# Layer 1's feed-forward network of a two-layer decoder, put into one written order

## The chip, the core and the metric

The kernel runs on one core of a Trainium2 chip. Such a core has engines that work side by side, each through a queue of its own, in order: TensorE (PE in the profile; PEld is its weight load), VectorE (DVE), ScalarE (ACT), GpSimd (POOL), and SyncE (SP), which issues the DMA transfers. They wait for one another through semaphores. Data lie in SBUF (128 partitions); matmul results go to PSUM, which DVE and ACT read and POOL does not touch in this kernel.

The metric is the device time of one execution in microseconds (us), lower is better. Before the change it is 2464.19 us, the median of three runs (2464.09 to 2467.39).

## What is computed

A decoder of two layers on x of shape (2, 1024, 256): six sublayers, each followed by a residual addition and a layernorm without weights. The change concerns the last sublayer, a SwiGLU network of width 704 with fake-quantised activations and weights:

```python
def _act_fake_quant(x, clip_factor):
    scale = sigmoid(clip_factor) * max(abs(x)) / 127.0      # one scale for the whole tensor
    return clip(round(x / scale), -128.0, 127.0) * scale
...
xq = _act_fake_quant(x, clip_x[0])
gate = einsum('bsh,ih->bsi', xq, _weight_fake_quant(w_gate))
up = einsum('bsh,ih->bsi', xq, _weight_fake_quant(w_up))
h = _act_fake_quant(silu(gate) * up, clip_down[0])
return einsum('bsi,hi->bsh', h, _weight_fake_quant(w_down))
...
x = _layernorm(x + _L1_ffn_ref(x, ...))
```

Two maxima over whole tensors cut this into stages: nothing of the network can start before the largest |x| is known, and no part of h can be quantised before the largest |h| is.

## The kernel before

The 2048 tokens are four groups of 512 (`NG = 4`, `GT = 512`); a group lies as four tiles of 128 tokens by 256. The quantised weights were made ready much earlier (`wgu`, `wdT`, with integers in bf16), and the scales are multiplied in afterwards.

**The end of the cross-attention** (`l1_xattn`). Token tiles n = 0 to 15 go through a pipeline of steps: softmax, turning, mixing with the values, turning back, output projection. `output` (L1625 on) adds the residual into `res[g]` (L1637) and normalises a group in two parts, three tiles when the third is there and one at the end: bn_stats and aggregate on DVE (L178, L179), variance plus epsilon (L181), a power of -1/2 on POOL (L183), the scaling on DVE (L200), then the part's largest |x| into a column of `xm` (L1644). Only PE's order is written by hand there.

**The maximum of x** (`whole_scale`, L1679 to L1693): a maximum on DVE, a transpose on PE, a second maximum, a broadcast by a matmul, a scalar operation and a reciprocal.

**Gate and up** (L1730 to L1755). `quantised(g)` rounds a group in two halves: ACT multiplies by the reciprocal scale and adds 12582912, which rounds to an integer (L1718), and two DVE operations clip from both sides and give bf16 (`integers`, L1709 and L1710). Eight transposes on PE (L1724) and two copies (`evac`, L70 on DVE and L74 on ACT) give `xqT`. Then six chunks of 128 hidden features (the last has 64): four matmuls of 512 columns into a PSUM tile of two banks (`wide`, two buffers), gate into one bank and up into the other (L1738); silu on ACT with gate's scale (L1743); on DVE the product of up, its scale and the silu into `h` (L1747), and the chunk's largest |h| into a column of `hm` (L1751). `quantised(g + 1)` stands behind chunk 2 in the program. The order of the instructions on every engine is a planner's here, which may pull ready work ahead.

**Quantise and down** (L1756 to L1780). After `whole_scale` for h, each group: per chunk ACT rounds (L1768), DVE clips in two operations (L1709, L1710) into `hq`, PE multiplies four token tiles with 256 columns of `wdT` (L1771), summing over the six chunks into two `wide` tiles, of which half the columns are used. Then DVE multiplies the four sums by `srow` (L1777), POOL adds x (L1779, in the last group DVE), and `layernorm` follows: statistics on DVE, power on POOL, an offset on DVE (L191), four scaled tiles on ACT (L196). `store` (L1784) sends the group's 512 KB to memory from SP's queue.

Of the kernel before, what the change touches and what calls it, by code (L numbers as in the profile page):

```python
# [9 lines left out]
F32 = mybir.dt.float32  # L10
# [8 lines left out]
P = 128  # L19
B, S, D = 2, 1024, 256  # L20
T = B * S
NG = 4
# [11 lines left out]
class Decoder:  # L34
# [1493 lines left out]
    def l1_xattn(self):  # L1528
# [11 lines left out]
        self.xm = self.late.tile([P, 2 * NG], F32, name="xm")  # L1540
        with ExitStack() as s:
# [84 lines left out]
            def output(n):  # L1626
# [11 lines left out]
                if i == 2:  # L1638
                    new[g] = self.xp.tile([P, 4, D], F32, tag="x", name="xg")
                tiles = {2: range(3), 3: range(3, 4)}.get(i)  # L1640
                if tiles:
                    self.normalise(new[g], res[g], tiles)
                    k = 2 * g + i - 2
                    nc.vector.tensor_reduce(  # L1644
                        self.xm[:, k : k + 1], new[g][:, tiles.start : tiles.stop, :], AX.XY, ALU.max,
                        apply_absolute_value=True,
                    )
# [22 lines left out]
    def l1_ffn(self, out):  # L1670
# [4 lines left out]
        with ExitStack() as s:  # L1675
# [36 lines left out]
            def quantised(g):  # L1712

                v = self.rp.tile([P, 4, D], F32, tag="r", name="r")
                xq = two.tile([P, 4, D], BF16, name="xq")
                for k in range(0, 4, 2):
                    i = slice(k, k + 2)
                    nc.scalar.activation(v[:, i, :], self.x[g][:, i, :], AF.Identity, bias=magic, scale=rx)  # L1718
                    integers(xq[:, i, :], v[:, i, :])
                xqT = two.tile([P, 2, GT], BF16, name="xqT")  # L1720
                for c in range(2):
                    ps = self.ps_t.tile([P, 1024], BF16, tag="t", name="bankb")
                    for i in range(4):
                        nc.tensor.transpose(  # L1724
                            ps[:, i * P : (i + 1) * P], xq[:, i, c * P : (c + 1) * P], self.identb
                        )
                    self.evac(xqT[:, c, :], ps[:, 0:GT])
                return xqT

            xqT = quantised(0)  # L1730
            for g in range(NG):
                now = xqT
                for c in range(NI):
                    n = rows(c)
                    ps = self.wide()
                    for k, wT in enumerate((wgT, wuT)):
                        for d in range(2):
                            nc.tensor.matmul(  # L1738
                                ps[0:n, k, :], lhsT=wT[:, d, c * P : c * P + n], rhs=now[:, d, :],
                                start=d == 0, stop=d == 1,  # L1740
                            )
                    sl = two.tile([P, GT], F32, name="sl", bufs=3)
                    nc.scalar.activation(  # L1743
                        sl[0:n, :], ps[0:n, 0, :], AF.Silu, scale=sg[0:n, c : c + 1]
                    )
                    hv = h[0:n, c, g * GT : (g + 1) * GT]
# [3 lines left out]
                    k = c * NG + g  # L1750
                    nc.vector.tensor_reduce(  # L1751
                        hm[0:n, k : k + 1], hv, AX.X, ALU.max, apply_absolute_value=True
                    )
                    if c == 2 and g + 1 < NG:
                        xqT = quantised(g + 1)  # L1755
            sh, rh = whole_scale(hm, 1, "wsh")  # L1756
            nc.vector.tensor_scalar(self.srow, self.srow, sh, None, ALU.mult)

            for g in range(NG):
                hq = self.weight(None, 1, 2048)[:, 0, :].bitcast(BF16)[:, 0 : NI * GT].rearrange(  # L1760
# [80 lines left out]
```

## Time and profile before

| what | time |
|---|---|
| three runs, median (lowest to highest) | 2464.19 us (2464.09 to 2467.39) |
| the profiled execution | 2464.71 us |
| its span, first to last instruction | 2462.9 us |
| mean granted TensorE clock | 0.982 |
| up to the last tile's scaled x, all other sublayers | to 2369.6 us |
| FFN, from the maximum of x to that of h | 2369.6 to 2413.1 us |
| FFN, quantise and down, to the last group's first product with srow | 2413.1 to 2450.6 us |
| last group's layernorm and store | 2450.6 to 2462.9 us |

How to read the lines of the profile: an engine, a line of the program (a helper's line stands for all its callers: L70 and L74 are `evac`, L183 and L200 the layernorm), an operation, the tile written and the tiles read, shapes as partitions x elements with type, a count. In a timeline the first two numbers are the start and the length in us; instructions of one line that follow each other are merged, so that "2.08 ... x4" are four in 2.08 us together, and as they are pipelined each is longer than a fourth of it. In brackets stands how long the engine was idle before, and what it waited for. In a table of stretches each engine has its busy time and its number of instructions, PEclk is the granted share of TensorE's clock, then come the DMA engines' share and rate. A summary of one line of the program gives a count and the shortest, median and longest duration in ns.

Over the whole span PE is busy 2331.8 us (95%), DVE 1677.5 us, ACT 1110.8 us and POOL 911.3 us. In the FFN stages it is otherwise: between 2369.6 and 2413.1 us PE is busy 29.16 us and DVE 38.51 us.

### The profile page before, as it was taken

The numbers are of one execution on the slowest core, as the hardware profiler recorded it, in microseconds if no ns is written. First come the engines' busy times: TensorE is split into PE (matmuls) and PEld (weight loads), VectorE is DVE, ScalarE is ACT, GpSimd is POOL, SyncE is SP. The second block draws the span as 40 slices with busy tenths as digits, with TensorE's granted clock in tenths as the row PEclk, the third lists the DMA queues.
The fourth block names the chain that finished last, engine by engine and source line by source line (L and its number), as shares of the span: only waits on it lengthen the run. The fifth ranks groups of instructions, "written<-read, shape, count | busy, mean of one in ns | idle before, by whom it ended". The sixth has DMA issues, their size and how long they took to land. (4 is left out here: it accounts for less than half of the span.)

```text
span 2462.9 us, 37293 instructions
## 1 busy us (share of the span) xinstructions
PE 2331.8 (95%) x14062; PEld 1580.2 (64%) x14065; DVE 1677.5 (68%) x2916; ACT 1110.8 (45%) x1730; POOL 911.3 (37%) x747
## 2 busy tenths in 40 slices
PE   7999999999998999999999999999989999999974
PEld 3545545444545668899999999999734444444742
DVE  6888887888785334555555555545788687885786
ACT  4665565565563322233333333333156555664344
POOL 4666666566565222342343332332210001002412
PEclk9999999999999999999999999999999999999986
DMA  7888788688787001010010010100212121210001
GB/s 160 174 159 169 148 169 166 131 161 170 151 172 187 1 1 41 1 39 27 13 35 30 18 41 6 48 1 1 49 25 42 28 40 30 47 23 1 1 1 35
DMA packets 275667, 168.78 MB, mean 69 GB/s; under 512 B 47560, under 2 KB 262176, under 8 KB 275488
## 3 DMA queue, kind: packets, MB, share of 16 engines
q1 hardware_dynamic: 239072, 148.05, 28.6%
q10 hardware_dynamic: 36416, 18.36, 3.7%
q8 instruction: 111, 1.82, 0.3%
q14 instruction: 68, 0.56, 0.1%
HBM read 34.21 MB, written 2.10 MB: 15 GB/s over the span
## 5 line engine op out<-in xcount | busy, mean ns | idle before, releaser
L312 DVE TENSOR_REDUCE nm<-wide 128x1 f32<-128x1024 f32 x256 | 300.7, 1214 | 63.2 <-PE wide L297 62.3
L1186 DVE TENSOR_REDUCE most<-bank 128x1 f32<-128x512 f32 x476 | 300.4, 684 | 25.3 <-PE bank L1176 17.3
L1229 ACT ACTIVATE w<-wide 128x1024 f32<-128x1024 f32 x256 | 248.3, 1022 | 147.0 <-PE wide L1223 138.8
L297 PE MATMUL wide<-k,q 64*128 64x512 f32 x1024 | 271.5, 627 | 18.8 <-ACT p L317 17.4
L328 POOL TENSOR_SCALAR p<-p,sums 128x1024 f32<-128x1024 f32 x128 | 143.6, 1121 | 269.6 <-DVE sums L325 269.6
L379 PE MATMUL acc<-turned,v 128*64 128x256 f32 x2048 | 235.1, 382 | 2.2 <-ACT aoT L74 1.7
L379 PEld LDWEIGHTS acc<-turned,v 128*64 128x64 f32 x2048 | 142.6, 137 | 113.6 <-issue 30.7
L906 ACT ACTIVATE mhT<-mhT,cols 128x256 f32<-128x256 f32 (+1 forms) x256 | 143.3, 607 | 147.4 <-DVE mhT L934 105.0
L317 ACT ACTIVATE p<-wide,nm 128x1024 f32<-128x1024 f32 x128 | 142.8, 1116 | 144.9 <-DVE nm L312 118.2
L817 POOL TENSOR_TENSOR hs<-hs,mhT 128x1024 f32<-128x1024 f32 x31 | 102.5, 3307 | 241.6 <-DVE hs L815 241.6
L342 DVE STREAM_TRANSPOSE blocks<-p 128x1024 f32<-128x1024 f32 x128 | 158.0, 1234 | 43.0 <-DMA turned<-blocks 13.3
L297 PEld LDWEIGHTS wide<-k,q 64*128 64x128 f32 x1024 | 89.9, 187 | 146.1 <-issue 76.5
L183 POOL TENSOR_TENSOR rstd<-ve,nhalf 128x4 f32<-128x4 f32 (+2 forms) x28 | 26.1, 934 | 424.7 <-DVE ve L181 424.3
L917 PE MATMUL unit<-xT,w 128*128 128x256 f32 x768 | 182.3, 380 | 0.0
L974 DVE SCALAR_TENSOR_TENSOR r<-acc,gates,r 128x128 f32<-128x128 f32 x256 | 77.7, 345 | 140.4 <-PE acc L965 140.4
L342 DVE STREAM_TRANSPOSE blocks<-r 128x1024 f32<-128x1024 f32 x128 | 153.8, 1202 | 0.0
L917 PEld LDWEIGHTS unit<-xT,w 128*128 128x128 f32 x768 | 140.9, 190 | 16.9 <-issue 0.3
L328 POOL TENSOR_SCALAR r<-r,sums 128x1024 f32<-128x1024 f32 x128 | 143.6, 1122 | 0.0
L317 ACT ACTIVATE r<-wide,nm 128x1024 f32<-128x1024 f32 x128 | 142.2, 1111 | 1.1 <-DVE nm L312 0.9
L1243 PE MATMUL acc<-w,v 128*32 128x512 f32 x1024 | 137.2, 608 | 0.0
L1176 PE MATMUL bank<-kst,qst 64*128 64x512 f32 x476 | 125.9, 459 | 11.8 <-DVE most L1186 11.8
L362 POOL COPY turned<-blocks 32x1024 f32<-32x1024 f32 x128 | 132.0, 1031 | 4.0 <-DVE blocks L342 0.3
(333 smaller groups left out, 4479.3 us busy)
## 6 DMA issues: line engine op xcount, KB each, us to landing
turned<-blocks SPq DMA_DIRECT2D x636, 128.0 KB, 2.8
turned<-blocks ACTq DMA_DIRECT2D x132, 128.0 KB, 3.1
w<-in_L_ffn_W SPq DMA_DIRECT2D x16, 1024.0 KB, 5.3
q<-q SPq DMA_DIRECT2D x64, 128.0 KB, 2.3
k<-k SPq DMA_DIRECT2D x32, 128.0 KB, 2.6
qst<-qh SPq DMA_DIRECT2D x48, 64.0 KB, 2.4
qst<-ql SPq DMA_DIRECT2D x48, 64.0 KB, 2.4
kst<-kh SPq DMA_DIRECT2D x48, 64.0 KB
```

The lines of the kernel that those rows point to most:

```text
L297: nc.tensor.matmul(sc[h][:, kb, :], lhsT=q[rows, qi, at : at + P], rhs=k[rows, ki, :], start=True, stop=True,)
L312: nc.vector.tensor_reduce(nm, sc, AX.XY, ALU.max, negate=True)
L317: nc.scalar.activation(p, sc.rearrange("p a c -> p (a c)"), AF.Exp, bias=nm, accum_out=sums[:, 0, h : h + 1],)
L328: nc.gpsimd.tensor_scalar(p, p, sums[:, 1, h : h + 1], 1.0, ALU.mult, ALU.mult)
L342: nc.vector.transpose(blocks[m][:, :, h, qt, :], p.rearrange("p (j q) -> p j q", q=32))
L362: nc.gpsimd.tensor_copy(b, a)
L379: nc.tensor.matmul(av[own[h], 0:256].rearrange("p (t i q) -> p i t q", t=2, i=4), lhsT=vals[u][:, kt, own[h]], rhs=p[:, h], start=kt == 0, ...
L906: nc.scalar.activation(hT[:, f, cols], hT[:, f, cols], AF.Relu, bias=self.cols[:, col : col + 1])
L917: nc.tensor.matmul(v[:, m, :], lhsT=up[e][k][:, f : f + P], rhs=self.halves[g][k], start=k in (1, 2, 5) and m == 0, stop=True, skip_group_ ...
L1186: nc.vector.tensor_reduce(most[n][:, kb, qt, h : h + 1], sc[a], AX.X, ALU.max, negate=True)
L1229: nc.scalar.activation(slot[:, k, :], ps[k].rearrange("p a q -> p (a q)"), AF.Exp, scale=0.25)
L1243: nc.tensor.matmul(mixed[n][o : o + 32, :], lhsT=vals[b][:, kt, 17 * h : 17 * h + 32], rhs=pT[:, a, :], start=kt == 0, stop=kt == 7, tile_ ...
```

## The change

1. **Cross-attention's end.** The last group is normalised in three parts (two tiles, one, one) instead of two; `xm` has a ninth column.
2. **One written order.** All of the FFN's instructions on PE, DVE, ACT and POOL, from the first rounding to the last layernorm, are issued in the program's order.
3. **Rounding x.** `quantised(g)` becomes `rounded` (ACT; in groups 1 to 3 also one clip from both sides on POOL), `clipped` (DVE: in those groups one operation that subtracts 12582912 and gives bf16) and `turned` (transposes, copy of the first half on DVE, of the second on ACT). For group g + 1 the six parts stand behind the six chunks of group g.
4. **Shared products.** In two of six chunks (1 and 4; in the last group 0 and 2) ACT scales up from PSUM into `h` and POOL multiplies by the silu, instead of one DVE product. The chunk's maximum stands two chunks later in all groups (`late`).
5. **Down.** The sums of a group take one `wide` tile. The previous group's `finish` is spread over the six chunks: products and adds (0, 1), statistics (2, 3), scaling and store of two tiles each (4, 5).
6. **Tail.** In the last group POOL adds x to two tiles and DVE to two, the statistics begin with the latter, ACT scales the first half and DVE the second; every group is stored in two DMAs of 256 KB.

```diff
-        self.xm = self.late.tile([P, 2 * NG], F32, name="xm")
+        self.xm = self.late.tile([P, 2 * NG + 1], F32, name="xm")
...
                 nc.vector.tensor_tensor(res[g][:, i, :], ps, self.x[g][:, i, :], ALU.add)
-                if i == 2:
-                    new[g] = self.xp.tile([P, 4, D], F32, tag="x", name="xg")
-                tiles = {2: range(3), 3: range(3, 4)}.get(i)
+                parts = {2: range(3), 3: range(3, 4)}
+                if g == NG - 1:
+                    parts = {1: range(2), 2: range(2, 3), 3: range(3, 4)}
+                tiles = parts.get(i)
                 if tiles:
+                    if tiles.start == 0:
+                        new[g] = self.xp.tile([P, 4, D], F32, tag="x", name="xg")
                     self.normalise(new[g], res[g], tiles)
-                    k = 2 * g + i - 2
+                    k = 2 * NG if i == 1 else 2 * g + i - 2
                     nc.vector.tensor_reduce(
                         self.xm[:, k : k + 1], new[g][:, tiles.start : tiles.stop, :], AX.XY, ALU.max,
                         apply_absolute_value=True,
...
                 nc.vector.tensor_scalar(out, v, MAGIC + QMAX, MAGIC, ALU.min, ALU.subtract)
                 nc.vector.tensor_scalar(out, out, -QMAX - 1.0, None, ALU.max)
...
+            vs, xqs, xqTs = {}, {}, {}
+            def rounded(g, k):
+                if k == 0:
+                    vs[g] = self.rp.tile([P, 4, D], F32, tag="r", name="r")
+                    xqs[g] = two.tile([P, 4, D], BF16, name="xq")
+                i = slice(2 * k, 2 * k + 2)
+                nc.scalar.activation(
+                    vs[g][:, i, :], self.x[g][:, i, :], AF.Identity, bias=magic, scale=rx
+                )
+                if g:
+                    v = vs[g][:, i, :]
+                    nc.gpsimd.tensor_scalar(v, v, MAGIC + QMAX, MAGIC - QMAX - 1.0, ALU.min, ALU.max)
+            def clipped(g, k):
+                i = slice(2 * k, 2 * k + 2)
+                if g:
+                    nc.vector.tensor_scalar(xqs[g][:, i, :], vs[g][:, i, :], MAGIC, None, ALU.subtract)
+                else:
+                    integers(xqs[g][:, i, :], vs[g][:, i, :])
+            def turned(g, c):
+                if c == 0:
+                    xqTs[g] = two.tile([P, 2, GT], BF16, name="xqT")
+                ps = self.ps_t.tile([P, 1024], BF16, tag="t", name="bankb")
+                for i in range(4):
+                    nc.tensor.transpose(
+                        ps[:, i * P : (i + 1) * P], xqs[g][:, i, c * P : (c + 1) * P], self.identb
+                    )
+                self.evac(xqTs[g][:, c, :], ps[:, 0:GT], by=nc.scalar if c else nc.vector)
+            shared = lambda g, c: c in ((0, 2) if g == NG - 1 else (1, 4))
+            late = []
+            def largest(g, c):
+                n, k = rows(c), c * NG + g
+                nc.vector.tensor_reduce(
+                    hm[0:n, k : k + 1], h[0:n, c, g * GT : (g + 1) * GT], AX.X, ALU.max,
+                    apply_absolute_value=True,
+                )
+            def hidden(g, c):
+                n = rows(c)
+                ps = self.wide()
+                for k, wT in enumerate((wgT, wuT)):
+                    for d in range(2):
+                        nc.tensor.matmul(
+                            ps[0:n, k, :], lhsT=wT[:, d, c * P : c * P + n], rhs=xqTs[g][:, d, :],
+                            start=d == 0, stop=d == 1,
                         )
...
+                sl = two.tile([P, GT], F32, name="sl", bufs=3)
+                nc.scalar.activation(sl[0:n, :], ps[0:n, 0, :], AF.Silu, scale=sg[0:n, c : c + 1])
+                hv = h[0:n, c, g * GT : (g + 1) * GT]
+                if shared(g, c):
+                    nc.scalar.activation(hv, ps[0:n, 1, :], AF.Identity, scale=su[0:n, c : c + 1])
+                    nc.gpsimd.tensor_tensor(hv, hv, sl[0:n, :], ALU.mult)
+                else:
                     nc.vector.scalar_tensor_tensor(
                         hv, ps[0:n, 1, :], su[0:n, c : c + 1], sl[0:n, :], ALU.mult, ALU.mult
                     )
...
+            hqs, sums, res, mvs, rstds = {}, {}, {}, {}, {}
+            def quantised(g, c):
+                n = rows(c)
+                hv = h[0:n, c, g * GT : (g + 1) * GT]
+                if c == 0:
+                    hqs[g] = self.weight(None, 1, 2048)[:, 0, :].bitcast(BF16)[:, 0 : NI * GT].rearrange(
+                        "p (c q) -> p c q", c=NI
+                    )
+                nc.scalar.activation(hv, hv, AF.Identity, bias=magic[0:n, :], scale=rh[0:n, :])
+                integers(hqs[g][0:n, c, :], hv)
+            def down(g, c):
+                n = rows(c)
+                if c == 0:
+                    sums[g] = self.wide().rearrange("p a (i d) -> p (a i) d", d=D)
                 for i in range(4):
+                    nc.tensor.matmul(
+                        sums[g][:, i, :], lhsT=hqs[g][0:n, c, i * P : (i + 1) * P],
+                        rhs=self.wdT[0:n, c, :], start=c == 0 and i % 2 == 0, stop=True,
+                        skip_group_check=True,
+                    )
+            def added(g, i, by):
+                if i == 0:
+                    res[g] = self.rp.tile([P, 4, D], F32, tag="r", name="r")
+                r = res[g][:, i, :]
+                nc.vector.tensor_tensor(r, sums[g][:, i, :], self.srow, ALU.mult)
+                by.tensor_tensor(r, r, self.x[g][:, i, :], ALU.add)
+            def weighed(g, i):
+                if g not in mvs:
+                    mvs[g] = self.sm.tile([P, 4, 2], F32, tag="mv", name="mv")
+                st = self.sm.tile([P, 6], F32, tag="st", name="st")
+                nc.vector.bn_stats(st, res[g][:, i, :])
+                nc.vector.bn_aggr(mvs[g][:, i, :], st)
+            def powers(g):
+                ve = self.sm.tile([P, 4], F32, tag="ve", name="ve")
+                nc.vector.tensor_scalar(ve, mvs[g][:, :, 1], EPS, None, ALU.add)
+                rstds[g] = self.sm.tile([P, 4], F32, tag="rstd", name="rstd")
+                nc.gpsimd.tensor_tensor(rstds[g], ve, self.nhalf, ALU.pow)
+            def written(g, half):
+                i = slice(2 * half, 2 * half + 2)
+                if half == 0:
+                    self.x[g] = self.xp.tile([P, 4, D], F32, tag="x", name="xg")
+                by = nc.vector if half and g == NG - 1 else nc.scalar
+                self.scaled(
+                    self.x[g], res[g], range(2 * half, 2 * half + 2), mvs[g][:, i, :],
+                    rstds[g][:, i], by,
+                )
+                b, h = divmod(g, 2)
+                nc.sync.dma_start(
+                    out[b, h * GT : (h + 1) * GT, :].rearrange("(i p) d -> p i d", p=P)[:, i, :],
+                    self.x[g][:, i, :],
+                )
+            def finish(g, c):
+                if c < 2:
+                    for i in range(2 * c, 2 * c + 2):
+                        added(g, i, nc.gpsimd)
+                elif c < 4:
+                    for i in range(2 * c - 4, 2 * c - 2):
+                        weighed(g, i)
+                    if c == 3:
+                        powers(g)
+                else:
+                    written(g, c - 4)
+            engines = {
+                mybir.EngineType.PE, mybir.EngineType.DVE, mybir.EngineType.Activation,
+                mybir.EngineType.Pool,
+            }
+            with self.tc.manual_schedule(engines=engines):
+                for k in range(2):
+                    rounded(0, k)
+                    clipped(0, k)
+                for c in range(2):
+                    turned(0, c)
+                for g in range(NG):
+                    for c in range(NI):
+                        hidden(g, c)
+                        late.append((g, c))
+                        while len(late) > 2:
+                            largest(*late.pop(0))
+                        if g + 1 < NG:
+                            if c < 2:
+                                rounded(g + 1, c)
+                            elif c < 4:
+                                clipped(g + 1, c - 2)
+                            else:
+                                turned(g + 1, c - 4)
+                while late:
+                    largest(*late.pop(0))
+                sh, rh = whole_scale(hm, 1, "wsh")
+                steps = [(g, c) for g in range(NG) for c in range(NI)]
+                for n, (g, c) in enumerate(steps):
+                    quantised(g, c)
+                    if n == 0:
+                        nc.vector.tensor_scalar(self.srow, self.srow, sh, None, ALU.mult)
+                    down(g, c)
+                    if g:
+                        finish(g - 1, c)
+                g = NG - 1
+                for i in range(4):
+                    added(g, i, nc.gpsimd if i < 2 else nc.vector)
+                for i in (2, 3, 0, 1):
+                    weighed(g, i)
+                powers(g)
+                for half in range(2):
+                    written(g, half)
```

Of the lines taken away, those of the FFN are left out here: they are `quantised`, the two loops over groups and `store`, printed above.

More of the change, by code (lines that the diff above doesn't have):

```diff
@@ L1710, in integers @@
                 nc.vector.tensor_scalar(out, out, -QMAX - 1.0, None, ALU.max)
[L1712 to L1725, printed above, removed]
-                        )
-                    self.evac(xqT[:, c, :], ps[:, 0:GT])
-                return xqT
@@ L1730, in l1_ffn @@
[L1730 to L1746, printed above, removed]
+            vs, xqs, xqTs = {}, {}, {}
@@ L1749, in l1_ffn @@
                     )
-                    k = c * NG + g
-                    nc.vector.tensor_reduce(
-                        hm[0:n, k : k + 1], hv, AX.X, ALU.max, apply_absolute_value=True
-                    )
[L1754 to L1760, printed above, removed]
-                    "p (c q) -> p c q", c=NI
-                )
-                ps = [self.wide(), self.wide()]
-                sums = [ps[i // 2][:, i % 2, 0:D] for i in range(4)]
-                for c in range(NI):
-                    n = rows(c)
-                    hv = h[0:n, c, g * GT : (g + 1) * GT]
-                    nc.scalar.activation(hv, hv, AF.Identity, bias=magic[0:n, :], scale=rh[0:n, :])
-                    integers(hq[0:n, c, :], hv)
-                    for i in range(4):
-                        nc.tensor.matmul(
-                            sums[i], lhsT=hq[0:n, c, i * P : (i + 1) * P], rhs=self.wdT[0:n, c, :],
-                            start=c == 0, stop=c == NI - 1,
-                        )
-                r = self.rp.tile([P, 4, D], F32, tag="r", name="r")
-                for i in range(4):
-                    nc.vector.tensor_tensor(r[:, i, :], sums[i], self.srow, ALU.mult)
-                    by = nc.vector if g == NG - 1 else nc.gpsimd
-                    by.tensor_tensor(r[:, i, :], r[:, i, :], self.x[g][:, i, :], ALU.add)
-                self.store(out, g, self.layernorm(r, nc.scalar))
@@ L1782, in store @@
-    def store(self, out, g, x):
-        b, h = divmod(g, 2)
-        self.nc.sync.dma_start(
-            out[b, h * GT : (h + 1) * GT, :].rearrange("(i p) d -> p i d", p=P), x
-        )
+            hqs, sums, res, mvs, rstds = {}, {}, {}, {}, {}
[5 more added lines that the diff above has]
+                        "p (c q) -> p c q", c=NI
+                    )
+                nc.scalar.activation(hv, hv, AF.Identity, bias=magic[0:n, :], scale=rh[0:n, :])
+                integers(hqs[g][0:n, c, :], hv)
```

## The prediction

> **What bounds the kernel now.** The change reaches only the last 97 us of the span, so I read the stage table of those first, then the chain of waits through them, then the timeline row by row. The stages are layer 1's FFN up to the whole-tensor maximum (A: quantise x, gate and up products), from there to the last down product (B), and the tail.
>
> ```profile
> core 0: us, PE busy (x) PEld busy (x) DVE busy (x) ACT busy (x) POOL busy (x), PEclk, DMA share, GB/s
> 2369.60:2413.10 43.50, 29.16 (x128) 12.98 (x131) 38.51 (x74) 25.50 (x37) 0.00 (x0) 0.88 0.00 1
> 2413.10:2450.60 37.50, 21.31 (x98) 12.44 (x99) 25.56 (x96) 23.25 (x36) 11.51 (x15) 0.65 0.10 33
> 2450.60:2462.90 12.30, 0.44 (x3) 0.00 (x0) 4.75 (x18) 2.07 (x4) 1.01 (x1) 0.50 0.22 73
> ```
>
> DVE is busy 89% of A while POOL does nothing: that is what the change works on. But a busy share is not a bound. The timeline of A's last group shows the loop behind it:
>
> ```profile
> 2404.49 0.59 PE L1738 MATMUL wide<-xqT,w_gateT 128*128 128x512 bf16 x2 [0.70 <-DVE h L1747]
> 2405.55 0.69 ACT L1743 ACTIVATE sl<-wide,sc_w_gate 128x512 f32<-128x512 f32 x1 [1.04 <-remote]
> 2406.40 1.49 DVE L1747 SCALAR_TENSOR_TENSOR h<-wide,sc_w_up,sl 128x512 f32<-128x512 f32 x2
> 2407.18 0.59 PE L1738 MATMUL wide<-xqT,w_gateT 128*128 128x512 bf16 x2 [0.81 <-DVE h L1747]
> 2407.80 1.27 DVE L1751 TENSOR_REDUCE hm<-h 128x1 f32<-128x512 f32 x2
> ```
>
> A chunk's silu starts 1.06 after its first matmul, the product 0.85 later, and the matmuls that reuse its PSUM buffer 0.78 after that: 2.69 for a buffer, two buffers, 1.35 a chunk. DVE's own work is about the same (0.66 a product and 0.59 a maximum, spaced as in these rows). So A is bound by latency as much as by DVE, and what counts in a fixed order is who waits behind whom.
>
> In B, ACT and DVE wait on each other around each layernorm:
>
> ```profile
> 2427.28 0.16 DVE L191 SCALAR_TENSOR_TENSOR off<-mv,rstd 128x4 f32<-128x4 f32 x1 [0.91 <-POOL rstd L183]
> 2427.47 2.08 ACT L196 ACTIVATE xg<-r,off,rstd 128x256 f32<-128x256 f32 x4 [2.29 <-DVE off L191]
> 2429.45 5.03 ACT L1768 ACTIVATE h<-h,magic,wsh 128x512 f32<-128x512 f32 x7
> ```
>
> ACT had quantised five or more chunks ahead before its layernorm stood in the queue; the next quantisation starts 1.98 after the first scaled tile. Tails start at 2421.49, 2431.61, 2441.13, 2450.65 (first product with srow): 9.7 us a group.
>
> Last, DVE and POOL exclude each other, in rows from earlier stages:
>
> ```profile
> 2303.43 0.95 POOL L1564 MEMSET lxp<- 128x1024 f32 x1 [1.37 <-PE bank L1588]
> 2303.76 0.65 DVE L181 TENSOR_SCALAR ve<-mv 128x3 f32<-128x3 f32 x1
> L1094 DVE TENSOR_SCALAR xg<-w x4: 419/679/1490, 1756.1 to 1758.8; 128x512 int32<-128x512 int32 x4
> L1095 POOL TENSOR_TENSOR xg<-w,xg x2: 1382/1416/1450, 1756.6 to 1758.0; 128x512 f32<-128x512 f32 x2
> ```
>
> A DVE scalar operation from SBUF to SBUF that takes 0.16 or 0.42 alone lasts 0.65 or 1.49 when a POOL instruction is already running: it ends at the POOL instruction's end (2304.41 against 2304.38) or some 0.28 later. Products out of PSUM, maxima and bn_stats beside POOL do not stretch (bn_stats 0.43 beside L1779).
>
> **Stage A after the change.** Out go 8 of 24 DVE products (0.66 each: 5.3) and, in three groups, one of two clipping operations per half (0.25 x 6: 1.5). In come 8 scaled copies on ACT (0.58 apart, as two silus that took 1.27), and on POOL 8 products and 6 clips. POOL's 128x512 product is 1.27 (L824), its clip lies between 0.43 (128x256, L1386) and 1.12 (128x1024, L328), I take 0.6. The maximum of a chunk stands two chunks later, so POOL's 1.27 is covered; without that cover each shared chunk would cost it. The row is L824's 1.27 against DVE's 0.74. [...]
>
> Now the written order, one middle group, t = 0 at chunk 0's first matmul, shared chunks 1 and 4. ACT: silu 0 1.06, rounding 1.64 (0.70 apart), silu 1 2.34, scaled copy 1 2.92, rounding 3.50, silu 2 4.20, silu 3 4.78. DVE: product 0 1.91; product 2 5.05, maximum 0 5.71, clip 6.30 (0.38), product 3 6.68, maximum 1 7.34, clip 7.93 to 8.35. PE: chunk 4 at 5.83 (5.05 + 0.78), done 6.69. Behind it in PE's queue stand the next group's transposes, which need both clips: 8.41 to 8.85, and chunk 5 is queued behind them: 8.85, not 7.46 when its buffer is free. Silu 5 9.91, product 5 10.76. The second transposes end at 10.15; their copy is ACT's, behind silu 5: 10.49 to 11.08. The next chunk 0 has its second matmul at 11.15, so its effective start is 10.94. Groups start at 2375.04, 2386.16, 2394.78 and 2402.75 now: 11.1, 8.6, 8.0. The first silu comes at about 2377.8 (rounding two halves from 2371.76, two copies, the 1.28 table load; 2378.08 now), an effective start of 2376.75. Then 3 x 10.94, and the last group (shared 0 and 2, nothing to prepare): product 1 3.07, product 3 5.76, product 5 8.45 by the same steps, then the last three maxima end at 10.98. End 2420.6 against 2413.13: **+7.4**. Bounds: groups at 8.0 give -1.4; PE at half clock, whose matmuls start 0.43 apart instead of 0.215 (as at 2376.27), adds 2.2 to a group's chain, +14 in all. The granted clock is 1.00 from 2386 on and the longest PE gap that I find above is 1.7, so I take full speed. [...]
>
> **Stage B.** Per chunk DVE needs 0.70 (0.46 + 0.24). Group 0 runs at ACT's pace, 0.72 a chunk: group 1 starts 5.4 after the first quantisation. In each later group the previous group's layernorm stands between chunks, t = 0 at the first clip. Without exclusion: chunks 0 and 1 carry two srow products each (0.35): 2.80. Chunk 2 0.70 and two stats with their aggregates (0.46 + 0.10, dependent): 4.6; chunk 3 the same and the variance: 6.5. POOL's power: off 1.40 later (2425.88 to 2427.28): 7.9. There comes the **new wait**: two scaled tiles stand in ACT's queue ahead of chunk 5's quantisation. Off to ACT 0.19, two tiles 1.0, quantisation 0.82, 0.03: DVE waits 2.04 for chunk 5's input. It clips (0.70), writes the second off, and waits 2.04 again, for the next group's chunk 0. Period 12.7. PE stands behind DVE all that time.
> With exclusion: add 0 runs 1.28 to 2.00, so chunk 1's first clip ends 2.28; add 1 then holds until 2.86, the second clip ends 3.01; chunk 2 loses the same to adds 2 and 3 and its stats start at 5.24 instead of 3.50. With the power as well, off is at 9.85 and the period 14.6. The rows say that this exclusion is there; I take it. From the first quantisation: 5.4 + 2 x 14.6 + 12.6 (to chunk 5's clip) + 1.1 (last matmuls) = 48.4, against 35.45 (2415.20 to 2450.65): **+13.0**. Without exclusion 5.4 + 2 x 12.7 + 10.6 + 1.1 = 42.5: +7.0. Far end: the waits vanish and DVE alone sets it, 5.4 + 3 x 7.75 + 1.1 = 29.7: -5.7 (7.75 = 4.2 clips + 1.4 products + 1.7 stats + 0.4).
>
> Two edits of B cost nothing: the sums take one PSUM buffer of two, so the next group's matmuls no longer wait for srow products (1.6 us of PE idle, beside DVE work anyway), and the stores become eight of 256 KB on SP, whose queue holds nothing else here.
>
> **Before and after them.** The last cross-attention group is normalised in 2 + 1 + 1 tiles instead of 3 + 1. Now, 3 scaled tiles (0.98), a 768-wide maximum (0.86) and a power of 0.86 stand before the last tile; after, one tile (0.33), a 256-wide maximum (0.33) and a power of 0.56: **-1.4**. Up to -2.1 if the last residual goes ahead of the scaling, +0.5 if the extra two-tile scaling (0.66) delays L1608's reciprocal, behind which the last transposes wait. Tail: adds split over POOL and DVE save nothing sure (two-input adds exclude each other); the halves put the store's start two ACT tiles earlier but add a second DMA on SP: power at 5.0 after the first product as now, second half issued at 8.0 instead of 8.4, a smaller transfer: **-0.6**, between -1.5 and +0.5 (a second issue, 0.37).
>
> **Sum:** -1.4 + 7.4 + 13.0 - 0.6 = +18.4 on the span of 2462.9: 2481.3. The profiled execution was 2464.71, 1.8 more than its span and 0.5 over the median of 2464.19. Against the median: **2482.6**.
>
> **Rivals.** (1) The waits are there but POOL's adds do not hold up DVE (their gaps let it through): 18.4 - 6.0 = +12.4, 2476.6. For: bn_stats slips by; against: the 1.49 row.
> (2) Faster: DVE is the bound, as its 89% suggests, and the waits fall into time in which buffers run ahead. A loses 5.3 + 1.5, B 5.7, the ends 2.0: 2449.7. Its place is A: it decides if a group takes under 8.3 us there, as groups 1 and 2 do now with the full DVE work. Against: chunk 5 behind transposes behind the second clip.
> (3) The written order doesn't bind ACT (quantisations still run ahead), so B costs nothing while A loses half: about 2466. Nothing in the profile speaks for it.
>
> **Chances.** A measurement of this kernel tells 0.2%, 4.9 us, from no change. Forecast 0.52, rival 1 0.22, rival 2 0.18, rival 3 0.08. The likeliest case alone: 2475 to 2490. The range takes in rival 1 and rival 3 and stops short of most of rival 2: 2459 to 2491. Slower 0.75 (forecast, rival 1, a little of 3), same 0.07, faster 0.18.
>
> **What would show it.** Group starts in A about 11 apart, with PE idle before the transposes and released by DVE's clip; six waits of 2 us of DVE's clip for ACT's quantisation in B; clips in B above 0.42 and 0.28 on average, beside POOL's adds; tails' first products 13 to 15 apart. Groups at 8 in A, or clips in B that wait for nothing, would prove me wrong.

## The result, and the profile after

| | median us | runs | lowest to highest |
|---|---|---|---|
| before | 2467.39 | 6 | 2464.09 to 2469.83 |
| after | 2484.15 | 6 | 2480.24 to 2488.28 |

The ratio is 1.0063, with a 95% interval of 1.005 to 1.0075. The changed kernel is slower, by 16.8 us between the two medians.

The two profiled executions differ by more: 2464.71 before, 2488.28 after. Of those 23.6 us, 8.2 have gathered before any instruction that the change touches has run: the last but one output product of the cross-attention (L1634) starts at 2361.48 in one and at 2369.71 in the other, at the end of the same sequence of instructions; the first part that the change alters, a variance of two tiles on DVE, comes at 2370.09. So the change is read stage by stage, each by its own length:

| stage, and the rows that bound it | before | after | difference | forecast |
|---|---|---|---|---|
| end of cross-attention: last L1634 to first reduction into wsx | 6.20 | 5.12 | -1.08 | -1.4 |
| A: reduction into wsx to reduction into wsh | 43.55 | 50.30 | +6.75 | +7.4 |
| scale of h: to its first rounding | 2.04 | 2.14 | +0.10 | 0 |
| B: first rounding of h to the last group's first product with srow | 35.45 | 46.59 | +11.14 | +13.0 |
| tail: to the end of the span | 12.25 | 10.71 | -1.54 | -0.6 |
| sum | | | +15.4 | +18.4 |

The stage table of the changed kernel, with the columns of the one before (busy time of each engine in each stretch, instructions in brackets):

```profile
core 0: us, PE busy (x) PEld busy (x) DVE busy (x) ACT busy (x) POOL busy (x), PEclk, DMA share, GB/s
2376.70:2427.00 50.30, 31.45 (x131) 12.34 (x131) 31.71 (x61) 29.13 (x45) 13.81 (x14) 0.87 0.00 1
2427.00:2475.70 48.70, 22.49 (x99) 10.61 (x99) 33.03 (x99) 23.41 (x36) 12.83 (x15) 0.57 0.08 27
2475.70:2486.50 10.80, 0.05 (x1) 0.00 (x0) 5.36 (x18) 1.25 (x3) 2.60 (x3) 0.50 0.22 73
```

A is the row to look at. The change took 6.8 us of work off DVE (38.51 to 31.71) and DVE's share of the stage fell from 89% to 63%, yet the stage became 6.8 us longer. In B the same number of DVE instructions, give or take three, is busy 7.5 us longer (25.56 to 33.03).

The timeline of the second group of A shows what holds it (start, length, engine, line; in brackets the idle time before it and what ended that):

```profile
2399.95 0.59 PE L1764 MATMUL wide<-xqT,w_gateT 128*128 128x512 bf16 x2 [1.04 <-DVE h L1775]
...
2400.73 0.75 DVE L1775 SCALAR_TENSOR_TENSOR h<-wide,sc_w_up,sl 128x512 f32<-128x512 f32 x1
...
2401.99 0.42 DVE L1733 TENSOR_SCALAR xq<-r 128x512 bf16<-128x512 f32 x1
...
2402.46 0.28 PE L1742 MATMUL bankb<-identb,xq 128*128 128x128 bf16 x2 [1.30 <-DVE xq L1733]
2402.68 0.86 PE L1764 MATMUL wide<-xqT,w_gateT 128*64 128x512 bf16 x2
...
2403.33 1.06 PE L1764 MATMUL wide<-xqT,w_upT 128*64 128x512 bf16 x2
...
2404.43 0.68 ACT L1769 ACTIVATE sl<-wide,sc_w_gate 64x512 f32<-64x512 f32 x1 [2.09 <-PE wide L1764]
...
2405.63 0.58 PE L1764 MATMUL wide<-xqT,w_gateT 128*128 128x512 bf16 x1 [0.27 <-ACT xqT L74]
```

PE stands still until DVE's second clip (L1733) lets the transposes go, and chunk 5 comes out of the queue behind them (gate at 2402.68, up at 2403.33), though chunk 3's product, which frees its buffer, has ended at 2401.48. The wait of 1.30 with this releaser is in each of the three groups that prepare a next one. Their first silus start at 2384.33, 2395.28, 2406.81 and 2417.34: 10.95, 11.53 and 10.53 apart, against 9.14, 8.62 and 7.98 before.

The timeline of B's second group, in the same columns:

```profile
2435.67 1.59 POOL L1809 TENSOR_TENSOR r<-r,xg 128x256 f32<-128x256 f32 x2 [13.34 <-DVE r L1808]
2435.84 0.84 DVE L1712 TENSOR_SCALAR w<-h 128x512 bf16<-128x512 f32 x1
2436.71 0.70 DVE L1713 TENSOR_SCALAR w<-w 128x512 bf16<-128x512 bf16 x1
...
2440.55 0.39 DVE L1712 TENSOR_SCALAR w<-h 128x512 bf16<-128x512 f32 x1
2440.98 0.29 DVE L1713 TENSOR_SCALAR w<-w 128x512 bf16<-128x512 bf16 x1
...
2443.80 0.16 DVE L191 SCALAR_TENSOR_TENSOR off<-mv,rstd 128x2 f32<-128x2 f32 x1 [0.58 <-POOL rstd L1822]
2443.99 1.09 ACT L196 ACTIVATE xg<-r,off,rstd 128x256 f32<-128x256 f32 x2 [6.93 <-DVE off L191]
2444.99 0.80 ACT L1789 ACTIVATE h<-h,magic,wsh 64x512 f32<-64x512 f32 x1
...
2445.82 0.42 DVE L1712 TENSOR_SCALAR w<-h 64x512 bf16<-64x512 f32 x1 [1.86 <-ACT h L1789]
```

The two operations of a clip take 0.84 and 0.70 while POOL adds, and 0.39 and 0.29 when it does not: this is the exclusion of the prediction, called the lock below. Then ACT sits idle for 6.93, its scaled tiles first in its queue, until off is there, rounds h only after them, and DVE waits 1.86 for that. Over the whole stage DVE waited for the rounding 10.2 us in six places, one of them the start; before it was 0.6, once.

### The profile page after: what moved, and what is told of

It reads as the page before. It is cut to its first block, busy times and chain, and to the rows that moved or that the text cites. A ratio compares the mean times of both kernels' runs of the same rounds, so it can differ in the third digit from the quotient of the medians.

```text
span 2486.5 us, 37322 instructions
## 1 busy us (share of the span) xinstructions
PE 2343.3 (94%) x14065; PEld 1580.1 (64%) x14065; DVE 1678.9 (68%) x2907; ACT 1114.2 (45%) x1736; POOL 927.6 (37%) x764
## 5 line engine op out<-in xcount | busy, mean ns | idle before, releaser
L817 POOL TENSOR_TENSOR hs<-hs,mhT 128x1024 f32<-128x1024 f32 x31 | 102.5, 3307 | 240.2 <-DVE hs L815 240.2
L183 POOL TENSOR_TENSOR rstd<-ve,nhalf 128x4 f32<-128x4 f32 (+3 forms) x25 | 22.3, 893 | 415.1 <-DVE ve L181 414.7
```

## The experiments

The rows without a median are single runs; they are read by stage length, since the kernel before, run beside them, gave 2465 to 2477 us. A and B are bounded as above. "Written" and "planner" say who sets the order of the instructions on each engine.

B needs care. Its first stretch, up to the first product with `srow`, differs between kernels whose code for B is the same: 5.97 in the changed kernel, 6.73 in e3, 6.97 in e10 and 7.18 in e5, where PE was at half clock for 4.45, 5.99, 6.60 and 7.18 of it. The rest of B, three groups, is 40.62, 40.61, 40.53 and 40.27 there. So differences of B under 1.2 are read from the three groups alone.

| kernel | order | products shared | A | groups of A | B | median us |
|---|---|---|---|---|---|---|
| before | planner | no | 43.55 | 9.14, 8.62, 7.98 | 35.45 | 2467.39 |
| after | written | yes | 50.30 | 10.95, 11.53, 10.53 | 46.59 | 2484.15 |
| e1_act_ahead | written | yes | 49.85 | 11.49, 10.53, 10.53 | 39.02 | |
| e2_no_adds | written | yes | 50.29 | 10.94, 11.52, 10.53 | 41.54 | |
| e3_early | written | yes | 47.85 | 8.36, 11.45, 9.04 | 47.34 | |
| e4_planner | planner | yes | 48.72 | 8.57, 10.32, 10.31 | 32.69 | |
| e5_unshared | written | no | 47.61 | 10.38, 9.98, 9.98 | 47.45 | |
| e6_dve_adds | written | yes | 50.31 | 10.96, 10.53, 11.52 | 47.14 | |
| e7_ahead_dve | written | yes | 50.31 | 10.96, 10.53, 11.53 | 38.34 | |
| e10_early_pool | written | yes | 54.96 | 12.17, 12.47, 11.33 | 47.50 | |
| e11_hand_best | written | no | 44.70 | 8.04, 9.08, 9.04 | 38.87 | |
| e9_planner_unshared | planner | no | 42.96 | 9.20, 8.12, 8.12 | 31.33 | 2461.28 |
| e12_planner_dve | planner | no | 42.88 | 9.13, 8.12, 8.11 | 32.52 | 2462.52 |

**e1_act_ahead**: B's waits for ACT. The rounding is taken out of `quantised` and written two chunks ahead, so that no scaled tile stands in front of the rounding that DVE needs next.

```
+                for k in range(2):
+                    risen(*steps[k])
                 for n, (g, c) in enumerate(steps):
+                    if n + 2 < len(steps):
+                        risen(*steps[n + 2])
                     quantised(g, c)
```

> Stage B only: ACT rounds h two chunks ahead of DVE's clips, so the two scaled tiles of a layernorm half no longer stand in ACT's queue before the next chunk's rounding. If the queue order costs what the trace of the changed kernel shows (five waits of DVE's clip for ACT's rounding, 1.86 us each), B, from the first rounding of h to the last group's first product with srow, falls from 46.6 us by about 9.3 to 37.4. Rival: the wait only moves (to the power on POOL or to the matmuls) and B stays above 43.

B went from 46.59 to 39.02, a gain of 7.6. Its groups come 10.6 apart instead of 14.1: 3.5 a group, where two waits of 1.86 make 3.7. The three groups together gained 8.8 (40.62 to 31.84), near the 9.3 expected; the first stretch became 1.2 longer, and PE was at half clock for the whole of it. Behind the off of the second group there is no wait any more; the rows in its timeline:

```profile
2445.85 0.16 DVE L191 SCALAR_TENSOR_TENSOR off<-mv,rstd 128x2 f32<-128x2 f32 x1 [0.58 <-POOL rstd L1826]
2445.93 0.41 DVE L1712 TENSOR_SCALAR w<-h 64x512 bf16<-64x512 f32 x1
```

The next clip starts 0.08 after off, not 2.02. All five waits of 1.86 are gone. So the order in ACT's queue is the larger part of B's loss.

**e2_no_adds**: the lock between POOL and DVE. POOL's adds of x are left out in groups 0 to 2 (the residual of these groups is missing from the result).

```
-                by.tensor_tensor(r, r, self.x[g][:, i, :], ALU.add)
+                if g == NG - 1:
+                    by.tensor_tensor(r, r, self.x[g][:, i, :], ALU.add)
```

> The additions of x on POOL in groups 0 to 2 are left out (the layernorms there are of the FFN's output alone). If POOL's adds hold up DVE's clips, the four clips per group that now last 0.83 and 0.70 us go back to 0.42 and 0.29, and B falls from 46.6 by 3 x 1.6 = 4.9 us. Rival 1 of the prediction (adds do not hold up DVE): B stays within 1 us of 46.6.

B became 41.54, 5.05 shorter, as expected, and no clip lasts longer than 0.43. This removes the adds, the lock and the statistics' wait for the adds together; the next kernel takes them apart.

**e6_dve_adds**: the same adds, on DVE.

```
-                        added(g, i, nc.gpsimd)
+                        added(g, i, nc.vector)
```

> One edit on the changed kernel: the adds of x on DVE instead of POOL in all groups. B was 46.6 with the adds on POOL and 41.5 without them. Theory 'in series': DVE's own adds stand ahead of the statistics in the same chain, 4 x 0.37 a group and three groups, so B is 45 to 46.5 and the lock is worth about as much as it costs to avoid it. Rival 'lock is the larger': the adds fall into the waits of 1.86 for ACT, B 41.5 to 43. Clips at 0.42 and 0.29 throughout in both.

B was 47.14: no gain, even 0.5 more than with POOL (also in the three groups alone, 41.11 against 40.62), and above the range of the theory in series. Clips are back at 0.42 and 0.29. The adds fall into no wait, as the five of 1.86 are all still there: each follows its product, on which it depends, and 0.45 pass from a product's start to its add's, where 0.34 pass between instructions that do not depend on each other:

```profile
2448.12 0.42 DVE L1808 TENSOR_TENSOR r<-wide,srow 128x256 f32<-128x256 f32 x1
...
2448.57 0.42 DVE L1809 TENSOR_TENSOR r<-r,xg 128x256 f32<-128x256 f32 x1
2448.91 0.42 DVE L1808 TENSOR_TENSOR r<-wide,srow 128x256 f32<-128x256 f32 x1
```

Twelve adds at 0.45 make 5.4; against e2, without them, the three groups are 5.55 longer. So the lock is real, 5 us of B, but not a reason to move the adds: on DVE they cost as much.

**e7_ahead_dve**: both edits of B together.

> In B, ACT's rounding of h two chunks ahead (as in e1_act_ahead, which gave 39.0 instead of 46.6) and the adds of x on DVE instead of POOL. Without the adds alone B was 41.5, so the two gains together, 7.6 and 5.1, would give 34. Theory 'independent costs': the adds cost DVE 4 x 0.35 a group instead of the lock, three groups: 34 + 4.2 = 38, hardly below 39.0, with clips at 0.42 and 0.29 throughout. Theory 'the adds fill time in which DVE waits for its own results': 34 to 35.5.

B was 38.34, near the 38 of the theory of independent costs. But the 0.7 that it is under e1 isn't a gain of the adds. The first product with `srow`, in e1 and then in e7:

```profile
2437.21 0.76 DVE L1812 TENSOR_TENSOR r<-wide,srow 128x256 f32<-128x256 f32 x2 [1.35 <-PE wide L1802]
2430.36 0.42 DVE L1812 TENSOR_TENSOR r<-wide,srow 128x256 f32<-128x256 f32 x1 [0.21 <-PE wide L1802]
```

In e1 DVE waits 1.35 for PE, which was at half clock for the whole first stretch (7.18), in e7 0.21, with 4.59 of 6.04 at half clock. The three groups behind it are longer in e7, 32.30 against 31.84: here too the adds on DVE cost 0.5 more than on POOL.

**e3_early**: A's place of the next group's preparation. Rounding, clips and transposes are written two chunks earlier, `prepare(g * NI + c + 2)`, which does for chunk c what the changed kernel does at c + 2.

```
-                        if g + 1 < NG:
-                            if c < 2:
-                                rounded(g + 1, c)
...
+                        prepare(g * NI + c + 2)
```

> Stage A only: the six parts that prepare the next group stand two chunks earlier, so that the transposes come after chunks 2 and 3 and their clips after chunks 0 and 1. If chunk 5 and the next chunk 0 are late because of the transposes behind the second clip and ACT's copy behind silu 5, groups start 8.0 to 8.8 us apart instead of 10.5 to 11.5, and A (from the maximum of x to that of h, now 50.3 us) falls to 41 to 43. Rival: ACT, with the scaled copies, is the bound; groups stay above 10.

A was 47.85, not 41 to 43. The first group shows the expected 8.36; the second took 11.45. In its timeline the second clip, written earlier, meets POOL's product:

```profile
2391.29 0.42 DVE L1733 TENSOR_SCALAR xq<-r 128x512 bf16<-128x512 f32 x1
...
2392.02 1.27 POOL L1773 TENSOR_TENSOR h<-h,sl 128x512 f32<-128x512 f32 x1 [1.84 <-ACT h L1772]
2392.22 1.34 DVE L1733 TENSOR_SCALAR xq<-r 128x512 bf16<-128x512 f32 x1
...
2393.62 0.28 PE L1742 MATMUL bankb<-identb,xq 128*128 128x128 bf16 x2 [1.57 <-DVE xq L1733]
```

The clip lasts 1.34 instead of 0.42 and ends 0.27 after the product; PE, idle for 1.57, then runs at half clock. The third group has the same long clip (1.34 at 2403.66) and takes 9.04. So the move was right, and worth 2.45 us of A, but the sharing of products puts a POOL instruction of 1.27 beside the clip. How much of the 11.45 is the long clip and how much the clock, this run doesn't tell; the third group's 9.04 is also what the last two groups of e11 take, whose clips last 0.42.

**e10_early_pool**: e3_early with that second operation of the clip on POOL.

```
-                    nc.vector.tensor_scalar(xqs[g][:, i, :], vs[g][:, i, :], MAGIC, None, ALU.subtract)
+                    nc.gpsimd.tensor_scalar(xqs[g][:, i, :], vs[g][:, i, :], MAGIC, None, ALU.subtract)
```

> The preparation of the next group two steps earlier (as in e3_early, A 47.9, groups 8.4, 11.5 and 9.0 apart) and the second of its clipping operations on POOL instead of DVE. Theory 'exclusion': in e3_early the slow middle group comes from the clip that lasted 1.34 instead of 0.42 beside POOL's product and from the PE gap and low clock behind it; with the clip on POOL the three groups are 8.3 to 9.1 apart and A is 43.5 to 45.5. Theory 'low clock whatever': the middle group stays above 11 and A at 47 to 48. If POOL itself becomes late (clip behind its 1.27 product) groups stay at 9.5 to 10.5, A 47 to 49.

All three theories missed: A was 54.96. The last one had the mechanism, POOL late with the clip, but not its size. The rows of the third group's preparation in the timeline:

```profile
2401.03 1.26 POOL L1773 TENSOR_TENSOR h<-h,sl 128x512 f32<-128x512 f32 x1 [0.26 <-ACT h L1772]
...
2402.27 1.48 POOL L1733 TENSOR_SCALAR xq<-r 128x512 bf16<-128x512 f32 x1
...
2403.81 0.40 PE L1742 MATMUL bankb<-identb,xq 128*128 128x128 bf16 x2 [2.69 <-POOL xq L1733]
2403.99 1.06 PE L1764 MATMUL wide<-xqT,w_gateT 128*128 128x512 bf16 x2
```

POOL needs 1.48 for an operation of this shape that writes bf16; its other clipping operation, from f32 to f32, takes 0.61. It queues behind the product, PE waits 2.69, and the matmuls that follow are 0.43 apart instead of 0.22. The edit cannot decide between the lock and the clock, since it makes a longer gap of its own.

**e5_unshared**: the written order with all products on DVE.

```
-            shared = lambda g, c: c in ((0, 2) if g == NG - 1 else (1, 4))
+            shared = lambda g, c: False
```

> Written order kept, all 24 products on DVE, no scaled copies on ACT, no products on POOL. Theory 'order': what a middle group of A costs is set by the second clip, behind which the transposes and chunk 5 stand; without the shared chunks DVE reaches that clip at about 7.1 instead of 8.35 after a group's first matmul, so groups come 9.5 to 9.9 apart instead of 10.5 to 11.5, and A is 46 to 47 (50.3 with the change, 43.5 before). Theory 'sharing': the products of ScalarE and GpSimd are the whole cost, the order none: groups 8.0 to 9.1 apart, A 43 to 44. If neither counts, A stays at 50. B stays at 46.6 in each.

A was 47.61 and the groups 10.38, 9.98 and 9.98. So even with DVE doing all 24 products A stays 4.1 us above before in the written order; sharing adds 2.7 to that. The theory of the order holds, its size a little above the range.

**e4_planner**: the written order is taken away, `ExitStack()` in the place of `manual_schedule`; all else stays.

> The same operations and the same program order, but without the fixed issue order: the planner may move them. If the order is what costs, A comes back to 40 to 44 us and B to 34 to 39, the whole near the kernel before. Rival: the operations themselves (POOL's share, the split halves) cost, and A plus B stay above 90 us of the present 96.9.

B fell from 46.59 to 32.69, better than expected and 2.8 under before. But A stayed at 48.72, where 40 to 44 were expected. The timeline shows a new wait:

```profile
2394.39 0.69 ACT L1769 ACTIVATE sl<-wide,sc_w_gate 128x512 f32<-128x512 f32 x1
...
2394.58 1.26 POOL L1773 TENSOR_TENSOR h<-h,sl 128x512 f32<-128x512 f32 x1 [3.89 <-ACT h L1772]
...
2395.88 0.69 DVE L1754 TENSOR_REDUCE hm<-h 128x1 f32<-128x512 f32 x1 [1.97 <-POOL h L1773]
2396.48 1.40 DVE L1775 SCALAR_TENSOR_TENSOR h<-wide,sc_w_up,sl 128x512 f32<-128x512 f32 x2
2397.27 0.59 PE L1764 MATMUL wide<-xqT,w_gateT 128*128 128x512 bf16 x2 [1.70 <-DVE h L1775]
```

Here the planner has put a shared chunk's maximum ahead of the next two products. DVE waits 1.97 for POOL, a product whose silu was ready at 2395.08 waits with it, and PE waits 1.70 for the buffers that these products free. The written order, with its lag of two chunks, does not have this wait; it has the other one.

**e9_planner_unshared**: e4 and e5 together.

> The order left to the planner (as in e4_planner: A 48.7, B 32.7) and no product shared; the layernorms in six parts, the halves of the tail and the 2+1+1 split stay. Theory 'sharing': in e4_planner DVE's maximum of a shared chunk stands ahead of the next products and waits 1.97 for POOL; without sharing A is 43 to 44.5 as before, B 32 to 33.5, tail 10 to 11, so the FFN from the maximum of x is 86 to 89 us against 93.3 before, and the time is 0.15 to 0.3% under before. Theory 'six parts in A': the preparation in parts costs A its 5 us whoever multiplies: A 47 to 49, and the time is before's within 0.2%.

2461.28 us (2458.96 to 2462.95, six runs) against 2469.46 for before, run beside it: ratio 0.9967, 95% interval 0.9955 to 0.9979. This is 0.3% under before and beats both kernels. Its stage table:

```profile
core 0: us, PE busy (x) PEld busy (x) DVE busy (x) ACT busy (x) POOL busy (x), PEclk, DMA share, GB/s
2371.60:2414.60 43.00, 28.72 (x128) 12.39 (x131) 37.29 (x69) 25.43 (x37) 3.91 (x6) 0.89 0.00 1
2414.60:2448.00 33.40, 23.23 (x99) 11.22 (x99) 27.39 (x98) 21.92 (x34) 13.00 (x15) 0.56 0.10 32
2448.00:2458.40 10.40, 0.01 (x1) 0.00 (x0) 5.24 (x18) 2.42 (x5) 2.42 (x3) 0.50 0.30 101
```

A is 42.96 and B 31.33 by the bounds of the first table, against 43.55 and 35.45; the tail is 1.9 shorter than before and the end of the cross-attention 1.1. Those four make -7.7 of the -8.2 measured. DVE is busy 37.3 us in A, 5.6 more than in the changed kernel, and the stage is 7.3 shorter. The theory of sharing holds: without it A is 5.8 shorter than in e4, though this edit takes away the wait for POOL and ACT's scaled copies together. In B it waits for ACT's rounding once, for 0.6, as before the change.

**e11_hand_best**: can the written order do as well? e5, e3 and e7 in one kernel.

> The written order kept, but with no product shared, the next group's preparation two steps earlier, ACT's rounding of h two chunks ahead, and the adds of x on DVE. Theory 'order': in A nothing stands behind a late clip any more, and DVE's own work sets a group: 6 x 0.66 products, 6 x 0.59 maxima, 2 x 0.42 clips and a 0.42 copy make 8.8 against 10.0 in e5_unshared; A 44 to 45.5, B 38 to 38.5 as in e7_ahead_dve. Rival 'low clock': the gap of PE before the transposes stays and so does half speed behind it: groups at 9.8 or more, A 47 or more. If A comes below 43.5 the written order is as good as the planner's and only its placing was at fault.

A was 44.70 and its last groups 9.08 and 9.04: the expected 44 to 45.5, so most of what the written order cost A lay in where the next group's preparation was put. PE still waits 1.29 for the second clip in two groups, but none comes to the 9.8 of the rival 'low clock'. B was 38.87, near e7's. Some 7 us of B are left against the planner; the next kernel bears on them.

**e12_planner_dve**: e9 with the adds of x on DVE (the edit of e6).

> e9_planner_unshared (A 43.0, B 31.3, time 0.9967 of before) with the adds of x on DVE instead of POOL. There two clips a group last 0.78 and 0.97 and one 0.48 beside POOL's adds, 1.1 more than alone, against 4 x 0.35 of adds on DVE. Theory 'even trade': B 31.5 to 32.5 and the time within 0.1% of e9_planner_unshared's. Rival 'POOL is worth it': DVE is the bound of B there (7.8 busy of 8.7), the adds come on top, B 33 to 35. Rival 'lock': B 29 to 31.

2462.52 us, ratio 0.9965 (0.9944 to 0.9985): not to be told from e9. B was 32.52, 1.2 more than in e9, at the upper end of the theory of an even trade. Here DVE has the same B work as in e7, adds included, and no add on POOL in either, yet groups come 8.6 to 9.0 apart instead of 10.8, with DVE busy 7.75 of 8.66 in a middle group instead of 9.28 of 10.76. The rows point to the order on DVE: the written one places each instruction right behind the one it depends on (0.45 from start to start, as in e6's rows, against 0.34), and the whole chain to off in one piece, while the planner puts clips of other chunks in between.

## Why the prediction came out as it did

The forecast was 2482.6 us and a loss of 18.4; measured were 2484.15 and 16.8 between the medians, 15.4 by stages. All the signs were right, and the mechanisms of A and B were those forecast; that A's total came so close is in part luck. By its steps:

**A, +7.4 forecast, +6.75 measured.** The chain was followed for a middle group, with t = 0 lying 1.06 before its first silu. The second and third groups of A, against it:

| step | forecast | second group | third group |
|---|---|---|---|
| end of the second clip | 8.35 | 8.19 | 8.17 |
| silu 5 | 9.91 | 10.21 | 9.54 |
| second matmul of the next group | 11.15 | 11.41 | 10.74 |

The third group ran at full clock and the second did not. So the chain at full speed was taken 0.4 too long: the clip 0.2, and 0.2 the transposes, of which four were put behind the second clip where two stood (0.22 from the first of them to chunk 5, at 2402.46 and 2402.68). What gave it back is the clock, which the forecast took to be full ("the longest PE gap that I find above is 1.7, so I take full speed"). That was the author's estimate: in earlier stages before, gaps of 1.73 and 2.36 at full clock brought no drop (PE back at 478.89 and 486.71), but here one of 1.30, with 1.04 before it, was followed by half clock. A group takes 10.53 at full speed, the second took 11.53, and the first 10.95, as its first 1.5 us fell before the rise of the clock (at 2385.86; its second silu comes 0.41 later than in the other two). The three make 33.0 us (3 x 10.94 = 32.8). The first silu comes 0.6 earlier than forecast, and from the last group's first silu to the end it is 9.72 (9.98).

**B, +13.0 forecast, +11.14 measured.** Both causes are there: in the three groups e1 is worth 8.8 and e2 5.1. Together, which no run shows, they would make 46.6 - 13.9 = 32.7, below the 35.45 of before (and what e4 takes, 32.69), so these two are enough to explain the loss. The mis-sized terms: a wait is 1.86 instead of 2.04, and there are five of them beside the start, not six; the lock costs 5.1 in three groups, not 6.0; a middle group takes 14.1 to 14.2 from first clip to first clip instead of 14.6 (off 9.52 after the first clip, forecast 9.85). The prediction's terms add up to 48.3, not 48.4. Rival 1, no lock, is refuted by the 0.84 and 0.70 of the clips and by e2.

**Rival 2 (DVE is the bound).** It hung on groups under 8.3 in A; they were 10.5 to 11.5. e5 and e9 show it from the other side: with all products back on DVE, A is shorter in either order, by 2.7 and by 5.8. DVE's 89% was not what held A, at least not alone: what it was relieved of came back as waits. **Rival 3** falls with e1: the written order does bind ACT.

**The tail, -0.6 forecast, -1.54 measured.** The step that failed is "second half issued at 8.0 instead of 8.4". The adds, as forecast, saved little: power starts 4.86 after the first product, 5.05 before. What the forecast passed over is that the second half's two tiles go to DVE (L200), beside ACT's two:

```profile
2481.78 0.74 DVE L200 TENSOR_SCALAR xg<-r,mv,rstd 128x256 f32<-128x256 f32 x2
2481.94 1.09 ACT L196 ACTIVATE xg<-r,off,rstd 128x256 f32<-128x256 f32 x2 [6.08 <-issue]
```

Both halves are ready 7.24 after the first product instead of 8.36, and the end follows 3.5 later instead of 3.9. **The end of the cross-attention, -1.4 forecast, -1.08 measured**: the two last tiles are normalised one after the other, and the second one's variance, and with it its power, stands in DVE's queue behind the first's scaling.

**What the forecast did not see** is that order and sharing each cost A by a mechanism of its own. e4 was expected to bring A back to 40 to 44 and did not. With sharing, A is 50.30 in the written order and 48.72 in the planner's; without, 47.61 and 42.96. Order alone costs 4.7 us, sharing alone 5.8, and both together 7.3, not the sum.

## What to carry to other kernels

Before work is taken from the busiest engine, follow one buffer through its loop: if the loop's latency is about as long as that engine's work, the helpers' own latency and the waits for them take back what the engine saves (in A a buffer's loop of 2.69 makes 1.35 a chunk, against 0.66 + 0.59 of DVE's work; 6.8 came off DVE, and the stage grew by 6.75). In an order written by hand, for each instruction ask what it makes the instructions behind it wait for: an early result that stands behind a late one in the same queue (the rounding behind scaled tiles, chunk 5 behind transposes) is where the time goes. And put independent work between instructions that depend on each other on one engine: on DVE such a pair started 0.45 apart in e6, independent ones 0.34.

## What the runs showed of the hardware

**PE fell to half clock behind a gap of 1.30 us.** Stretches of the changed kernel around the transposes at 2402.46, by the granted clock:

```profile
2402.00:2403.00 1.00, 0.54 (x4) 0.33 (x5) 1.00 (x4) 0.33 (x1) 0.58 (x1) 0.96 0.00 0
2403.00:2404.00 1.00, 1.00 (x4) 0.26 (x2) 0.33 (x1) 0.00 (x0) 0.68 (x1) 0.50 0.02 8
2404.00:2405.00 1.00, 1.00 (x6) 0.56 (x6) 0.00 (x0) 0.57 (x1) 0.00 (x0) 0.50 0.00 0
2405.00:2406.00 1.00, 0.73 (x2) 0.10 (x1) 0.86 (x2) 0.58 (x2) 0.00 (x0) 0.50 0.00 0
2406.00:2407.00 1.00, 1.00 (x5) 0.44 (x4) 0.48 (x1) 0.19 (x1) 0.00 (x0) 0.83 0.00 0
```

Half speed lasts from about 2402.9 to 2406.3, 3.4 us, and costs the group 1.0 (11.53 against 10.53). The gap of 1.30 has one of 1.04 shortly before it (idle up to 2399.95 in the first timeline). Both gaps stand in all three groups, but in the changed kernel the clock falls behind those of the second alone; groups of that length, 11.49 to 11.53, are the second in e2, the first in e1 and the third in e6 and e7, whose A is the same code. In the changed kernel the clock changed at 2375.62, 2385.86, 2402.93, 2406.34 and 2426.82, each time a multiple of 3.41 us after the last. In the 3.41 us before the drop, which hold 1.30 and part of the other gap, PE was busy 1.68; the third group's two gaps are spread over two such stretches, with 1.89 and 1.90 busy. So it may be that it counts how a gap falls into these stretches; that is the author's reading, and no run tests it. The length of a gap alone doesn't settle it: the gap of 2.36 ahead of L157 brought no drop before (clock 1.00 up to 796.09), and in the changed kernel the same gap (PE back at 490.45) was followed by half clock from 491.46 to 494.88. What share of busy time is too little stays open: e4's single gaps of 1.7, one every 5.2 us, brought no drop, though PE was busy only 1.62 and 1.54 in two stretches of 3.41 (2399.61 to 2403.02, 2409.85 to 2413.26).

**DVE's clips took longer beside POOL's adds.** In B a clip of 0.42 becomes 0.84 beside two adds that take 1.59 together, and the operation behind it 0.70 instead of 0.29. The clip ends at 2436.68, 0.28 after the first add (2436.40), and the second add, already under way, takes 0.91 instead of 0.72. Two-input operations (TENSOR_TENSOR) show it too: before, DVE's L815 takes 1.22 in the median and 2.28 at 1675.83, where POOL's L826 is running; L816, which starts at 1678.15, 0.11 ahead of POOL's L817, keeps its 1.23. In the tail of the changed kernel DVE's two adds took 0.46 and 0.49 beside POOL's (0.41 before, with POOL idle). In A, products out of PSUM and maxima of one input kept their 0.75 and 0.68 beside POOL's product of 1.27.

**POOL's clip into bf16 took 1.48**, against 0.61 for its clip of the same shape into f32 with two operations (e10). Whether the output type or the single operation makes it, no run here tells.
